# Attention weights turned within SBUF and divided after the value product

## The chip, the cores and the metric

The kernel runs on one core of a Trainium2 chip, in one launch. The metric is device time in microseconds, the median of the runs. A single profiled execution gives the trace; its span is the time from the first to the last instruction.

## What is computed

Two layers are applied to four images of 32 x 32 positions and 768 channels, in float32. Each layer normalises in 32 channel groups, runs multi-head attention with decomposed relative position terms (12 heads of 64 channels, 1024 queries and 1024 keys per image), projects, and adds the input. Cut to the attention, with S = 1024:

```python
q, k, v = (x_normed @ Wqkv)                     # per head: S x 64
bias = rel_h[..., :, None] + rel_w[..., None, :]   # from q and two small tables
scores = scale * q @ k.T + bias                 # S x S
attn = softmax(scores, axis=-1)
out = attn @ v
x = x + out @ Wproj + bproj
```

The second layer scales q once more before the position terms and has a bias on q, k and v.

## The kernel before

Data lie with channels on the 128 partitions. An image's attention is done by pairs of heads: head 0 of a pair is on partitions 0 to 63 and head 1 on 64 to 127. There are 8 image passes (2 layers, 4 images) of 6 pairs each, so 48 pairs, numbered g, and each pair has 8 units n of 128 queries. The main loop (L491) walks the 384 units in order. The order on TensorE (PE) is written by hand; the other engines' orders and the DMA queues are laid out by the framework's scheduler, and every engine works through its own order. DMAs from SyncE's queue (SP) are issued in order, and eight completion semaphores go round over all DMAs, so that one DMA waits for the eighth before it.

One turn of the loop does this on PE: the scores of the next unit (`scores`, L320: both heads, two blocks of 512 keys), a share of the waiting projection work (`take`, L464), at some units the value product (`weigh`), and the turning of new values (`turn_values`). The projection work is that of the next pair (`project_in`, L225, six groups of six matmuls for q, k and v) and the output projection (`project_out`, L425). Whatever has been put in the list `early` runs at the beginning of the next turn, for instance the position products (`positions`, tp, L276).

For one unit and head the softmax goes through five engines:

- POOL adds the two position terms into a score buffer sc (`biases`, L308), two units ahead.
- PE writes the scores to PSUM (s; three buffers).
- VectorE (DVE) adds both, negated, and keeps the minimum (L327, sm); this frees the PSUM buffer.
- ScalarE (ACT) takes the exponential and its sum (L331).
- DVE takes the reciprocal of the sums (L335), and POOL multiplies the block with it (L338).
- DVE transposes the block in squares of 32 by 32 into tb (L356).

After two units, SP writes tb of each head to DRAM (td, 1 MB, L359), and reads it back rearranged (pt, 1 MB, L360), so that keys lie on the partitions. pt holds 512 queries of one head in a single buffer per head. Every four units `weigh` multiplies with the values: 16 matmuls of 512 columns (8 key blocks, 2 heads; each float32 matmul is two instructions in the trace), and two copies from PSUM to attn (L379).

Score buffers (pool `sc`, six of 4 KB per partition) also hold v before it is turned (L218) and the result t of the position products (L280). ACT sends t to DRAM (tdr, L283); sixteen SP transfers read it back shifted (rel, L298), and POOL's bias sums of the next pair use it. The projection of v writes its columns in a changed order (L222), which the squares of the transposes ask for. PSUM has two further buffers (`ps_m`), in which projections, turned values, value products and outputs alternate.

Of the kernel before, what the change touches and what calls it, by code (L numbers as in the profile page):

```python
# [23 lines left out]
FP = mybir.dt.float32  # L28
AF = mybir.ActivationFunctionType
ALU = mybir.AluOpType  # L30

P = 128
B, HW, C = 4, 32, 768
S = HW * HW
NH, D = 12, 64
NC = C // P
NT = S // P
# [3 lines left out]
HALF = 512  # L41
# [7 lines left out]
def attention_blocks(ctx: ExitStack, tc: tile.TileContext, a: dict, out: bass.AP):  # L49
    nc = tc.nc  # L50
# [6 lines left out]
    apool = ctx.enter_context(tc.tile_pool(name="attn", bufs=6))  # L57
    qkpool = ctx.enter_context(tc.tile_pool(name="qk", bufs=2))
    vpool = ctx.enter_context(tc.tile_pool(name="v", bufs=2))
    scpool = ctx.enter_context(tc.tile_pool(name="sc", bufs=6))  # L60
    tbpool = ctx.enter_context(tc.tile_pool(name="tb", bufs=4))
    ptpool = ctx.enter_context(tc.tile_pool(name="pt", bufs=1))
    relpool = ctx.enter_context(tc.tile_pool(name="rel", bufs=2))
    iopool = ctx.enter_context(tc.tile_pool(name="io", bufs=4))
    small = ctx.enter_context(tc.tile_pool(name="small", bufs=4))
    dram = ctx.enter_context(tc.tile_pool(name="scratch", bufs=1, space=bass.MemoryType.DRAM))
    dram2 = ctx.enter_context(tc.tile_pool(name="scratch2", bufs=2, space=bass.MemoryType.DRAM))
# [9 lines left out]
    NPAIR = NI * NP  # L77
# [133 lines left out]
    def project_in(g, which, i):  # L211

        im, pair = divmod(g, NP)
        l = images[im][0]
        xn, w = xn_of[im], w_of[g, which]
        cols = slice(i * HALF, (i + 1) * HALF)
        if i == 0:
            pool, tag = (scpool, "sc") if which == 2 else (qkpool, "qk"[which])  # L218
            qkv_of[g, which] = pool.tile([P, S], FP, tag=tag, name=f"{'qkv'[which]}_{g}")
        to = qkv_of[g, which][:, cols]  # L220
        if which == 2:
            to = qkv_of[g, 2].rearrange("p (k j y) -> p y k j", y=4, k=NT)[:, 2 * i : 2 * i + 2]  # L222
        t = ps_m.tile([P, HALF], FP, tag="m", name=f"pj_{g}_{which}_{i}")
        for c in range(NC):
            nc.tensor.matmul(  # L225
                t, lhsT=w[:, c, :], rhs=xn[c][:, cols],
                start=(c == 0), stop=(c == NC - 1),
            )
            if c < NC - 1:
                yield True  # L230
        if which == 2:
            t = t.rearrange("p (y k j) -> p y k j", y=2, k=NT)
        bias = bqkv[:, which, pair : pair + 1]
        if which == 0:
            if l == 0:
                nc.scalar.activation(to, t, AF.Copy, scale=SCALE)  # L236
            else:
                nc.scalar.activation(to, t, AF.Identity, bias=bias, scale=SCALE * SCALE)  # L238
        elif l == 0:
            nc.vector.tensor_copy(to, t)  # L240
        else:
            nc.vector.tensor_scalar(to, t, bias, None, ALU.add)
        if which == 0:
            early.append(lambda: positions(g, i))
        if which == 2 and i == 1:
            late.extend([lambda: turn_values(g, 0), lambda: turn_values(g, 1)])
        if i == 1 and g + 1 < NPAIR:
            early.append(lambda: load_w(g + 1, which))
        if which == 2 and i == 1 and pair == NP - 1 and im + 1 < NI:
            early.extend([lambda: load_x(im + 1), lambda: norm_stats(im + 1)])  # L250
        yield True

    def turn_values(g, i):


        if i == 0:
            v_of[g] = vpool.tile([P, NT, P], FP, tag="v", name=f"v_{g}")
        t = ps_m.tile([P, 4, P], FP, tag="m", name=f"vt_{g}_{i}")
        for j in range(4):
            at = 4 * i + j  # L260
            nc.tensor.transpose(t[:, j, :], qkv_of[g, 2][:, at * P : (at + 1) * P], ident)  # L261
        nc.scalar.copy(v_of[g][:, 4 * i : 4 * i + 4, :], t)  # L262

    def positions(g, i):
# [7 lines left out]
        for j in range(4):  # L272
            for h in range(2):
# [3 lines left out]
                    ps[:, h, j, :], lhsT=q[rows, at * P : (at + 1) * P], rhs=tabs[l][rows, :],  # L277
                    start=True, stop=True,
                )
        t = scpool.tile([P, 4, 2, P], FP, tag="sc", name=f"t_{g}_{i}")  # L280
        nc.scalar.copy(t, ps.rearrange("p h j r -> p j h r"))  # L281
        td = t_of[g]
        nc.scalar.dma_start(  # L283
# [14 lines left out]
                        nc.sync.dma_start(out=rel_of[g][32 * y : 32 * y + 32, h, ax, :, :], in_=src)  # L298


    sc_of, tb_of, pt_of, attn_of = {}, {}, {}, {}

    def biases(g, n):
        rel = rel_of[g]
        for h in range(2):
            sc = scpool.tile([P, HW, HW], FP, tag="sc", name=f"sc_{g}_{n}_{h}")
            sc_of[g, n, h] = sc
            nc.gpsimd.tensor_tensor(  # L308
                sc, rel[:, h, 0, n, :].unsqueeze(2).to_broadcast([P, HW, HW]),
                rel[:, h, 1, n, :].unsqueeze(1).to_broadcast([P, HW, HW]), ALU.add,  # L310
            )

    def scores(g, n):
        q, k = qkv_of[g, 0], qkv_of[g, 1]
        ps = [ps_s.tile([P, S], FP, tag="s", name=f"s_{g}_{n}_{h}") for h in range(2)]
        for i in range(2):
            cols = slice(i * HALF, (i + 1) * HALF)
            for h in range(2):
                rows = slice(h * D, (h + 1) * D)
                nc.tensor.matmul(  # L320
                    ps[h][:, cols], lhsT=q[rows, n * P : (n + 1) * P], rhs=k[rows, cols],
                    start=True, stop=True,
                )
        st = small.tile([P, 3, 2], FP, tag="sm", name=f"sm_{g}_{n}")
        for h in range(2):
            sc = sc_of[g, n, h].rearrange("p y x -> p (y x)")
            nc.vector.tensor_tensor_reduce(  # L327
                out=sc, in0=ps[h], in1=sc, scale=-1.0, scalar=BIG, op0=ALU.add, op1=ALU.min,
                accum_out=st[:, 0, h : h + 1],
            )  # L330
            nc.scalar.activation(  # L331
                sc, sc, AF.Exp, bias=st[:, 0, h : h + 1], scale=-1.0,
                accum_out=st[:, 1, h : h + 1],
            )
        nc.vector.reciprocal(st[:, 2, :], st[:, 1, :])  # L335
        for h in range(2):
            sc = sc_of[g, n, h].rearrange("p y x -> p (y x)")
            nc.gpsimd.tensor_scalar(sc, sc, st[:, 2, h : h + 1], 1.0, ALU.mult, ALU.mult)  # L338

    def turn(g, n):  # L340

        half, quarter, j = n // 4, n // 2 % 2, n % 2
        for h in range(2):
            if n % 4 == 0:
                pt_of[g, half, h] = ptpool.tile(  # L350
                    [P, 2, 4, NT, 2 * HW], FP, tag=f"pt{h}", name=f"pt_{g}_{half}_{h}"
                )
            if j == 0:
                tb_of[h] = tbpool.tile([P, HW, 2, HW], FP, tag="tb", name=f"tb_{g}_{n}_{h}")
            tb, pt = tb_of[h], pt_of[g, half, h]
            nc.vector.transpose(tb[:, :, j, :], sc_of[g, n, h])  # L356
            if j == 1:
                td = dram2.tile([P, S * 2], FP, tag=f"td{h}", name=f"td_{g}_{n}_{h}")
                nc.sync.dma_start(out=td, in_=tb.rearrange("p k n i -> p (k n i)"))  # L359
                nc.sync.dma_start(  # L360
                    out=pt[:, quarter].rearrange("p r k t -> p r (k t)"),
                    in_=td.rearrange("(r j) (y t) -> (j y) r t", r=4, y=4),
                )

    def weigh(g, half):
        if half == 0:
            attn_of[g] = apool.tile([P, S], FP, tag="attn", name=f"attn_{g}")
        av = ps_m.tile([P, HALF], FP, tag="m", name=f"av_{g}_{half}")
        for k in range(NT):
            for h in range(2):  # L370
                rows = slice(h * D, (h + 1) * D)
                nc.tensor.matmul(  # L372
                    av[rows, :], lhsT=v_of[g][:, k, rows],
                    rhs=pt_of[g, half, h][:, :, :, k, :].rearrange("p q r t -> p (q r) t"),
                    start=(k == 0), stop=(k == NT - 1),
                )
        for q in range(2):
            at = half * HALF + q * 2 * P
            nc.vector.tensor_copy(  # L379
                attn_of[g][:, at : at + 2 * P].rearrange("p (n r i) -> p r n i", n=2, r=4),  # L380
                av[:, q * 2 * P : (q + 1) * 2 * P].rearrange("p (r n i) -> p r n i", n=2, r=4),
            )

# [53 lines left out]

    early, late = [], []

    def run(todo):
        while todo:
            todo.pop(0)()
# [30 lines left out]
    with tc.manual_schedule(engines={mybir.EngineType.PE}):  # L477
# [13 lines left out]
        for at, (g, n) in enumerate(units):  # L491
# [12 lines left out]
            if end and pair == NP - 1 and n == 2:  # L504
                todo = put_out(im, 0, range(12))
            run(early)
            if at + 1 < len(units):
                scores(*units[at + 1])
            if at + 2 < len(units):
# [2 lines left out]
            del late[:1]  # L512
            turn(g, n)
            take(todo, -(-left(todo) // (NT - n)))
            if n % 4 == 1 and at > 4:
                weigh(*(units[at - 2][0], n // 4 ^ 1))
            run(ready)
        weigh(NPAIR - 1, 1)
        run(early)
        todo = put_out(NI - 1, 1, range(12))  # L520
        while todo:
# [49 lines left out]
```

## Time and profile before

| | |
|---|---|
| Median of 3 runs | 4029.03 us (4026.11 to 4030.14) |
| Profiled execution, its own time | 4009.88 us |
| Its span | 4008.2 us |
| Mean granted clock of TensorE | 0.98 |
| Busy share PE, DVE, POOL, ACT | 95%, 58%, 57%, 29% |
| Main DMA queue | 564720 packets, 1032.05 MB, 73.6% of 16 engines' span |

Groups of the trace are named by line, engine and operation, then output<-input. A group gives its count, its busy time in us and the mean of one in ns, then the idle time of the engine before it and who ended that. In the chain of waits each line gives start, length and what ran; "issue" is time in which the profile shows no wait. In timelines the numbers are start and length in us. SPq and ACTq are the issuing queues. A float32 matmul counts as two instructions, each with its weight load (PEld).

### The profile page before, as it was taken

The page shows a single profiled execution, that of the slowest core. Times are in us where ns is not written, and L with a number is a line of the kernel's source. Part 1 is how long each engine was busy: PE and PEld are TensorE (multiplying, and loading weights), DVE is VectorE, ACT ScalarE, POOL GpSimd, SP SyncE. Part 2 cuts the span into 40 slices and gives each one's busy share as a digit, 9 for nine tenths or more (in the row PEclk, how much of TensorE's full clock was granted, in tenths as well). Part 3 has the DMA queues.
Part 4 walks back from the last instruction along what each step waited for, and adds up shares of the span by engine and source line. Part 5 has one row for each costly group of instructions (what it writes and reads, how often), then busy time and mean ns, then how long its engine had stood idle before and what let it go on. Part 6 is the DMA issues. An engine that isn't in the chain of part 4 may idle for free.

```text
span 4008.2 us, 39298 instructions
## 1 busy us (share of the span) xinstructions
PE 3795.4 (95%) x13056; PEld 1577.2 (39%) x13056; DVE 2324.9 (58%) x3520; ACT 1150.5 (29%) x1848; POOL 2300.8 (57%) x1555
## 2 busy tenths in 40 slices
PE   7989899999999999999999998999999999999998
PEld 3334333433344334444344343433344343434332
DVE  4555655547565565656665566555665566546653
ACT  2233223322232222322232223323233222322320
POOL 4656556655666546656556565655556565556661
PEclk9999999999999999999999999999999999999998
DMA  4777777878787787877877787878877788778867
GB/s 166 247 260 266 284 257 278 299 248 290 257 288 276 260 300 253 295 268 278 285 275 277 266 298 280 278 251 288 301 264 265 266 287 305 261 248 283 288 250 244
DMA packets 615612, 1084.89 MB, mean 271 GB/s; under 512 B 234481, under 2 KB 295153, under 8 KB 566257
## 3 DMA queue, kind: packets, MB, share of 16 engines
q1 hardware_dynamic: 564720, 1032.05, 73.6%
q10 hardware_dynamic: 50688, 50.34, 3.7%
q8 instruction: 103, 1.69, 0.2%
q14 instruction: 101, 0.82, 0.1%
HBM read 578.92 MB, written 503.32 MB: 270 GB/s over the span
## 4 chain that ended last, share of the span: by engine, by line
PE 61%; DMA 11%; DVE 10%; POOL 6%; ACT 5%; issue 5%; SPq 1%; ACTq 0%; DVEq 0%; POOLq 0%
PE pj L225 20%; PE av L372 17%; PE s L320 11%; PE o L425 9%; DMA tdr<-t 8%; DVE tb L356 4%; ACT sc L331 4%; POOL sc L308 3%; POOL sc L338 3%; DVE sc L327 3%; PE tp L276 3%; DMA pt<-td 2%; DVE st L155 1%; ACT t L281 1%; PE vt L261 1%
## 5 line engine op out<-in xcount | busy, mean ns | idle before, releaser
L308 POOL TENSOR_TENSOR sc<-rel 128x1024 f32<-128x1024 f32 x768 | 1451.6, 1910 | 578.2 <-DMA tdr<-t 341.4
L225 PE MATMUL pj<-xn,w 128*128 128x512 f32 x3456 | 1581.4, 607 | 1.1 <-DVE xn L201 1.1
L331 ACT ACTIVATE sc<-sc,sm 128x1024 f32<-128x1024 f32 x768 | 878.6, 1145 | 2063.0 <-DVE sm L327 1558.6
L338 POOL TENSOR_SCALAR sc<-sc,sm 128x1024 f32<-128x1024 f32 x768 | 849.1, 1118 | 1063.1 <-DVE sm L335 1028.8
L356 DVE STREAM_TRANSPOSE tb<-sc 128x1024 f32<-128x1024 f32 x768 | 917.9, 1226 | 741.5 <-POOL sc L338 740.3
L225 PEld LDWEIGHTS pj<-xn,w 128*128 128x128 f32 x3456 | 640.3, 192 | 924.5 <-issue 908.9
L327 DVE CUSTOM_DVE_ANT_0 sc<-s,sc 128x1024 f32<-128x1024 f32 x768 | 905.8, 1214 | 159.3 <-PE s L320 155.8
L320 PE MATMUL s<-k,q 64*128 64x512 f32 x3072 | 844.7, 623 | 54.3 <-DVE sm L327 54.3
L372 PE MATMUL av<-pt,v 128*64 128x512 f32 x3072 | 706.9, 606 | 34.1 <-DMA pt<-td 10.2
L425 PE MATMUL o<-attn,wo 128*128 128x512 f32 x1152 | 537.6, 615 | 26.3 <-DVE res L432 21.2
L320 PEld LDWEIGHTS s<-k,q 64*128 64x128 f32 x3072 | 294.0, 189 | 461.0 <-issue 288.7
L372 PEld LDWEIGHTS av<-pt,v 128*64 128x64 f32 x3072 | 264.4, 139 | 462.6 <-issue 369.1
L425 PEld LDWEIGHTS o<-attn,wo 128*128 128x128 f32 x1152 | 213.2, 193 | 333.8 <-issue 272.2
L335 DVE RECIPROCAL sm<-sm 128x2 f32<-128x2 f32 x384 | 63.5, 165 | 441.5 <-ACT sc L331 441.5
L379 DVE COPY attn<-av 128x256 f32<-128x256 f32 x192 | 71.9, 416 | 251.1 <-PE av L372 251.0
L281 ACT COPY t<-tp 128x1024 f32<-128x1024 f32 x96 | 97.1, 1012 | 285.4 <-PE tp L276 277.9
L276 PE MATMUL tp<-tab,q 64*128 64x128 f32 x1536 | 111.6, 285 | 42.3 <-ACT q L238 20.9
L331 ACT ACTIVATION_READ_ACCUMULATOR sc<-sc,sm 128x1 f32 x768 | 143.2, 186 | 0.0
L276 PEld LDWEIGHTS tp<-tab,q 64*128 64x128 f32 x1536 | 93.3, 187 | 108.9 <-ACT q L236 40.5
L262 ACT COPY v<-vt 128x512 f32<-128x512 f32 x96 | 55.9, 583 | 219.4 <-PE vt L261 218.4
L261 PE MATMUL vt<-ident,v 128*128 128x128 f32 x384 | 60.0, 280 | 34.1 <-DVE res L432 28.8
L261 PEld LDWEIGHTS vt<-ident,v 128*128 128x128 f32 x384 | 46.1, 142 | 92.5 <-DVE res L432 40.4
(45 smaller groups left out, 655.7 us busy)
## 6 DMA issues: line engine op xcount, KB each, us to landing
td<-tb SPq DMA_DIRECT2D x384, 1024.0 KB, 6.1
pt<-td SPq DMA_DIRECT2D x384, 1024.0 KB, 7.2
w<-in_wqkv SPq DMA_DIRECT2D x144, 384.0 KB, 7.2
tdr<-t ACTq DMA_DIRECT2D x96, 512.0 KB, 7.6
rel<-tdr SPq DMA_DIRECT2D x768, 32.0 KB, 2.0
part<-res SPq DMA_DIRECT2D x96, 256.0 KB, 5.3
res<-part SPq DMA_DIRECT2D x96, 256.0 KB, 5.1
wo<-in_wo SPq DMA_DIRECT2D x84, 192.0 KB, 4.4
```

Source lines behind the costliest of these rows:

```text
L225: nc.tensor.matmul(t, lhsT=w[:, c, :], rhs=xn[c][:, cols], start=(c == 0), stop=(c == NC - 1),)
L261: nc.tensor.transpose(t[:, j, :], qkv_of[g, 2][:, at * P : (at + 1) * P], ident)
L276: nc.tensor.matmul(ps[:, h, j, :], lhsT=q[rows, at * P : (at + 1) * P], rhs=tabs[l][rows, :], start=True, stop=True,)
L281: nc.scalar.copy(t, ps.rearrange("p h j r -> p j h r"))
L308: nc.gpsimd.tensor_tensor(sc, rel[:, h, 0, n, :].unsqueeze(2).to_broadcast([P, HW, HW]), rel[:, h, 1, n, :].unsqueeze(1).to_broadcast([P, ...
L320: nc.tensor.matmul(ps[h][:, cols], lhsT=q[rows, n * P : (n + 1) * P], rhs=k[rows, cols], start=True, stop=True,)
L327: nc.vector.tensor_tensor_reduce(out=sc, in0=ps[h], in1=sc, scale=-1.0, scalar=BIG, op0=ALU.add, op1=ALU.min, accum_out=st[:, 0, h : h + 1],)
L331: nc.scalar.activation(sc, sc, AF.Exp, bias=st[:, 0, h : h + 1], scale=-1.0, accum_out=st[:, 1, h : h + 1],)
L338: nc.gpsimd.tensor_scalar(sc, sc, st[:, 2, h : h + 1], 1.0, ALU.mult, ALU.mult)
L356: nc.vector.transpose(tb[:, :, j, :], sc_of[g, n, h])
L372: nc.tensor.matmul(av[rows, :], lhsT=v_of[g][:, k, rows], rhs=pt_of[g, half, h][:, :, :, k, :].rearrange("p q r t -> p (q r) t"), start=(k ...
L425: nc.tensor.matmul(t, lhsT=w[:, c - c0, :], rhs=attn_of[im * NP + c][:, cols], start=(c == c0), stop=(c == c1 - 1),)
```

## The change

- The blocks are no longer divided before the value product. POOL's multiplication (L338) goes; the reciprocal is taken once per 256 queries over both heads. It is written to DRAM (rd) and read back onto all 64 partitions of each head (rb), and the value product is multiplied with it when it leaves PSUM.
- The transposed blocks no longer pass through DRAM. Both heads and two units share one tb; sixteen transfers of 32 rows by 4 KB move its four row blocks into the four row blocks of pt, within SBUF. pt now holds 256 queries of both heads, in two buffers.
- `weigh` works on 256 queries, every two units, with 16 matmuls of 256 columns and one multiplication.
- v is written in its own order. v and t have a pool of their own (`tmp`); `sc` has three buffers of both heads.
- From the second pair of an image on, the position products go to a list `later`, which runs one turn after `early` would.

```diff
-    scpool = ctx.enter_context(tc.tile_pool(name="sc", bufs=6))
-    tbpool = ctx.enter_context(tc.tile_pool(name="tb", bufs=4))
-    ptpool = ctx.enter_context(tc.tile_pool(name="pt", bufs=1))
+    scpool = ctx.enter_context(tc.tile_pool(name="sc", bufs=3))
+    tmppool = ctx.enter_context(tc.tile_pool(name="tmp", bufs=2))
+    tbpool = ctx.enter_context(tc.tile_pool(name="tb", bufs=2))
+    ptpool = ctx.enter_context(tc.tile_pool(name="pt", bufs=2))
+    rbpool = ctx.enter_context(tc.tile_pool(name="rb", bufs=3))
...
-            pool, tag = (scpool, "sc") if which == 2 else (qkpool, "qk"[which])
+            pool, tag = (tmppool, "tmp") if which == 2 else (qkpool, "qk"[which])
...
-        if which == 2:
-            to = qkv_of[g, 2].rearrange("p (k j y) -> p y k j", y=4, k=NT)[:, 2 * i : 2 * i + 2]
...
-            early.append(lambda: positions(g, i))
-        if which == 2 and i == 1:
-            late.extend([lambda: turn_values(g, 0), lambda: turn_values(g, 1)])
+            (later if pair else early).append(lambda: positions(g, i))
+        if which == 2:
+            late.append(lambda: turn_values(g, i))
...
-        t = scpool.tile([P, 4, 2, P], FP, tag="sc", name=f"t_{g}_{i}")
+        t = tmppool.tile([P, 4, 2, P], FP, tag="tmp", name=f"t_{g}_{i}")
...
-        nc.vector.reciprocal(st[:, 2, :], st[:, 1, :])
-        for h in range(2):
-            sc = sc_of[g, n, h].rearrange("p y x -> p (y x)")
-            nc.gpsimd.tensor_scalar(sc, sc, st[:, 2, h : h + 1], 1.0, ALU.mult, ALU.mult)
...
     def turn(g, n):
-            nc.vector.transpose(tb[:, :, j, :], sc_of[g, n, h])
-            if j == 1:
-                td = dram2.tile([P, S * 2], FP, tag=f"td{h}", name=f"td_{g}_{n}_{h}")
-                nc.sync.dma_start(out=td, in_=tb.rearrange("p k n i -> p (k n i)"))
-                nc.sync.dma_start(
-                    out=pt[:, quarter].rearrange("p r k t -> p r (k t)"),
-                    in_=td.rearrange("(r j) (y t) -> (j y) r t", r=4, y=4),
-                )
+        quarter, j = divmod(n, 2)
+        if j == 0:
+            tb_of[g, quarter] = tbpool.tile([P, 4, 2, NT, 2, HW], FP, tag="tb", name=f"tb_{g}_{n}")
+        tb = tb_of[g, quarter]
+        for h in range(2):
+            nc.vector.transpose(
+                tb[:, :, h, :, j, :].rearrange("p y k i -> p k y i"),
+                sc_of[g, n][:, h].rearrange("p (k y) x -> p k y x", y=4),
+            )
+        if j == 1:
+            pt = ptpool.tile([P, 4, 2, NT, 2 * HW], FP, tag="pt", name=f"pt_{g}_{quarter}")
+            st = st_of[g, quarter]
+            nc.vector.reciprocal(
+                st[:, 2].rearrange("p h n -> p (h n)"), st[:, 1].rearrange("p h n -> p (h n)")
+            )
+            rd = dram2.tile([2, 2 * P], FP, tag="rd", name=f"rd_{g}_{quarter}")
+            nc.sync.dma_start(
+                out=rd.rearrange("h (n p) -> p (h n)", p=P),
+                in_=st[:, 2].rearrange("p h n -> p (h n)"),
+            )
+            rb = rbpool.tile([P, 2 * P], FP, tag="rb", name=f"rb_{g}_{quarter}")
+            for y in range(4):
+                for r in range(4):
+                    nc.sync.dma_start(
+                        out=pt[32 * y : 32 * y + 32, r].rearrange("p h k t -> p (h k t)"),
+                        in_=tb[32 * r : 32 * r + 32, y].rearrange("p h k n i -> p (h k n i)"),
+                    )
+            for h in range(2):
+                nc.sync.dma_start(
+                    out=rb[h * D : (h + 1) * D, :], in_=rd[h : h + 1, :].to_broadcast([D, 2 * P])
+                )
 
-    def weigh(g, half):
+    def weigh(g, quarter):
...
-                    rhs=pt_of[g, half, h][:, :, :, k, :].rearrange("p q r t -> p (q r) t"),
+                    rhs=pt_of[g, quarter][:, :, h, k, :],
...
-        for q in range(2):
-            at = half * HALF + q * 2 * P
-            nc.vector.tensor_copy(...)
+        at = quarter * 2 * P
+        nc.vector.tensor_tensor(
+            attn_of[g][:, at : at + 2 * P].rearrange("p (n r i) -> p n r i", n=2, r=4),
+            av.rearrange("p (r n i) -> p n r i", n=2, r=4),
+            rb_of[g, quarter].rearrange("p (n r i) -> p n r i", n=2, r=4), ALU.mult,
+        )
...
             run(early)
+            early, later = later, early
...
-            if n % 4 == 1 and at > 4:
-                weigh(*(units[at - 2][0], n // 4 ^ 1))
+            if n % 2 == 1 and at > 2:
+                weigh(units[at - 2][0], units[at - 2][1] // 2)
```

More of the change, by code (lines that the diff above doesn't have):

```diff
@@ L230, in project_in @@
                 yield True
-        if which == 2:
-            t = t.rearrange("p (y k j) -> p y k j", y=2, k=NT)
         bias = bqkv[:, which, pair : pair + 1]
@@ L298, in positions @@
                         nc.sync.dma_start(out=rel_of[g][32 * y : 32 * y + 32, h, ax, :, :], in_=src)
-    sc_of, tb_of, pt_of, attn_of = {}, {}, {}, {}
+    sc_of, st_of, tb_of, pt_of, rb_of, attn_of = {}, {}, {}, {}, {}, {}
     def biases(g, n):
         rel = rel_of[g]
+        sc = scpool.tile([P, 2, HW, HW], FP, tag="sc", name=f"sc_{g}_{n}")
+        sc_of[g, n] = sc
         for h in range(2):
-            sc = scpool.tile([P, HW, HW], FP, tag="sc", name=f"sc_{g}_{n}_{h}")
-            sc_of[g, n, h] = sc
             nc.gpsimd.tensor_tensor(
-                sc, rel[:, h, 0, n, :].unsqueeze(2).to_broadcast([P, HW, HW]),
+                sc[:, h], rel[:, h, 0, n, :].unsqueeze(2).to_broadcast([P, HW, HW]),
                 rel[:, h, 1, n, :].unsqueeze(1).to_broadcast([P, HW, HW]), ALU.add,
@@ L323, in scores @@
                 )
-        st = small.tile([P, 3, 2], FP, tag="sm", name=f"sm_{g}_{n}")
+        if n % 2 == 0:
+            st_of[g, n // 2] = small.tile([P, 3, 2, 2], FP, tag="sm", name=f"sm_{g}_{n}")
+        st = st_of[g, n // 2]
         for h in range(2):
-            sc = sc_of[g, n, h].rearrange("p y x -> p (y x)")
+            sc = sc_of[g, n][:, h].rearrange("p y x -> p (y x)")
             nc.vector.tensor_tensor_reduce(
                 out=sc, in0=ps[h], in1=sc, scale=-1.0, scalar=BIG, op0=ALU.add, op1=ALU.min,
-                accum_out=st[:, 0, h : h + 1],
+                accum_out=st[:, 0, h, n % 2 : n % 2 + 1],
@@ L330, in scores @@
             )
             nc.scalar.activation(
-                sc, sc, AF.Exp, bias=st[:, 0, h : h + 1], scale=-1.0,
-                accum_out=st[:, 1, h : h + 1],
-            )
-        nc.vector.reciprocal(st[:, 2, :], st[:, 1, :])
-        for h in range(2):
[L337 to L347, printed above, removed]
-        for h in range(2):
-            if n % 4 == 0:
-                pt_of[g, half, h] = ptpool.tile(
-                    [P, 2, 4, NT, 2 * HW], FP, tag=f"pt{h}", name=f"pt_{g}_{half}_{h}"
-                )
[L353 to L356, printed above, removed]
-            if j == 1:
-                td = dram2.tile([P, S * 2], FP, tag=f"td{h}", name=f"td_{g}_{n}_{h}")
-                nc.sync.dma_start(out=td, in_=tb.rearrange("p k n i -> p (k n i)"))
-                nc.sync.dma_start(
-                    out=pt[:, quarter].rearrange("p r k t -> p r (k t)"),
-                    in_=td.rearrange("(r j) (y t) -> (j y) r t", r=4, y=4),
-                )
@@ L365, in weigh, with turn @@
-    def weigh(g, half):
-        if half == 0:
+                sc, sc, AF.Exp, bias=st[:, 0, h, n % 2 : n % 2 + 1], scale=-1.0,
+                accum_out=st[:, 1, h, n % 2 : n % 2 + 1],
+            )
+    def turn(g, n):
+        quarter, j = divmod(n, 2)
+        if j == 0:
+            tb_of[g, quarter] = tbpool.tile([P, 4, 2, NT, 2, HW], FP, tag="tb", name=f"tb_{g}_{n}")
+        tb = tb_of[g, quarter]
+        for h in range(2):
+            nc.vector.transpose(
[4 more added lines that the diff above has]
+            pt = ptpool.tile([P, 4, 2, NT, 2 * HW], FP, tag="pt", name=f"pt_{g}_{quarter}")
+            pt_of[g, quarter] = pt
+            st = st_of[g, quarter]
[8 more added lines that the diff above has]
+            rb = rbpool.tile([P, 2 * P], FP, tag="rb", name=f"rb_{g}_{quarter}")
+            rb_of[g, quarter] = rb
+            for y in range(4):
[7 more added lines that the diff above has]
+                    out=rb[h * D : (h + 1) * D, :], in_=rd[h : h + 1, :].to_broadcast([D, 2 * P])
+                )
@@ L367, in weigh @@
+    def weigh(g, quarter):
+        if quarter == 0:
             attn_of[g] = apool.tile([P, S], FP, tag="attn", name=f"attn_{g}")
-        av = ps_m.tile([P, HALF], FP, tag="m", name=f"av_{g}_{half}")
+        av = ps_m.tile([P, HALF], FP, tag="m", name=f"av_{g}_{quarter}")[:, : 2 * P]
         for k in range(NT):
@@ L373, in weigh @@
                     av[rows, :], lhsT=v_of[g][:, k, rows],
-                    rhs=pt_of[g, half, h][:, :, :, k, :].rearrange("p q r t -> p (q r) t"),
+                    rhs=pt_of[g, quarter][:, :, h, k, :],
                     start=(k == 0), stop=(k == NT - 1),
                 )
-        for q in range(2):
-            at = half * HALF + q * 2 * P
[L379 to L382, printed above, removed]
+        at = quarter * 2 * P
[4 more added lines that the diff above has]
+        )
     parts = [(im, p, o, i) for im in range(NI) for p in range(2) for o in range(NC) for i in range(2)]
@@ L437, in project_out @@
         yield True
-    early, late = [], []
+    early, later, late = [], [], []
     def run(todo):
@@ L514, in attention_blocks @@
             take(todo, -(-left(todo) // (NT - n)))
-            if n % 4 == 1 and at > 4:
-                weigh(*(units[at - 2][0], n // 4 ^ 1))
+            if n % 2 == 1 and at > 2:
+                weigh(units[at - 2][0], units[at - 2][1] // 2)
             run(ready)
-        weigh(NPAIR - 1, 1)
+        weigh(NPAIR - 1, 3)
         run(early)
```

## The prediction

> **What bounds the kernel now.** I read the page first (busy shares and groups), then the timeline of TensorE (PE) over the whole span, the chain of waits around one of its gaps, and the timeline of SP's queue. The page:
>
> ```profile
> PE 3795.4 (95%) x13056; PEld 1577.2 (39%) x13056; DVE 2324.9 (58%) x3520; ACT 1150.5 (29%) x1848; POOL 2300.8 (57%) x1555
> ...
> PE 61%; DMA 11%; DVE 10%; POOL 6%; ACT 5%; issue 5%; SPq 1%; ACTq 0%; DVEq 0%; POOLq 0%
> ...
> L338 POOL TENSOR_SCALAR sc<-sc,sm 128x1024 f32<-128x1024 f32 x768 | 849.1, 1118 | 1063.1 <-DVE sm L335 1028.8
> ...
> L356 DVE STREAM_TRANSPOSE tb<-sc 128x1024 f32<-128x1024 f32 x768 | 917.9, 1226 | 741.5 <-POOL sc L338 740.3
> ```
>
> PE is the bound, yet the chain that ended last lies on it for 61% only. POOL's 849 us of division matter for one reason: DVE's transposes wait 740 us for them. The timeline of PE shows what a unit costs (a unit is 128 queries of one head pair):
>
> ```profile
> 2034.53 7.09 PE L372 MATMUL av<-pt,v 128*64 128x512 f32 x32
> ...
> 2042.14 1.16 PE L276 MATMUL tp<-tab,q 64*128 64x128 f32 x16
> ...
> 2050.29 1.99 PE L320 MATMUL s<-k,q 64*128 64x512 f32 x8
> 2052.21 5.42 PE L225 MATMUL pj<-xn,w 128*128 128x512 f32 x12
> 2057.56 1.12 PE L320 MATMUL s<-k,q 64*128 64x512 f32 x2
> 2059.65 1.98 PE L320 MATMUL s<-k,q 64*128 64x512 f32 x6 [0.97 <-DVE sm L327]
> ```
>
> Start to start, undisturbed: scores 1.92 us, six projection matmuls 5.35, values of 512 queries 7.02 (16 pairs of instructions at 0.43, the two heads together, and 0.16 of change-over). At 2057.56 a score run stops after two of its eight instructions. The chain of waits there:
>
> ```profile
> 2047.52 1.24 ACT sc L331 x2
> 2048.77 3.64 issue
> 2052.41 1.91 POOL sc L308
> 2054.32 1.11 POOL sc L338
> ...
> 2055.45 1.13 DVE tb L356
> ...
> 2058.45 1.13 DVE sc L327
> ...
> 2059.65 1.98 PE s L320 x6
> ```
>
> POOL stands 3.64 us before a bias sum (its buffer is held by t until tdr lands at 2052.35); the division queues behind that sum, the transposes behind the division, the next scores' reduction behind the transposes, and PE behind that. Even without the 3.64 us, DVE's reduction repeats every 8.40 us (2005.23, 2013.63), against 1.92 + 5.35 = 7.27 on PE.
>
> I went through PE's whole timeline, subtracting the undisturbed pace from each run of matmuls. 160 runs lose over 1 us, 297 us together: 123 in scores behind L327, 43 where tp or vt follow at once on ACT's copy of q, 37 behind the output sums L432 and L434, 94 elsewhere. Of each about 0.2 is ordinary change-over, so 265 us are stalls, and a PE without them would end near 3743.
>
> **Removed.** The division (768 x 1118 ns on POOL) with its link in the chain. The transposes then wait for the exponential alone. In the same rows: reduction at 0, first exponential 1.33 to 2.48, transposes from about 2.6 to 5.0, a copy of 0.7: 5.7 us per unit instead of 8.4, below PE's 7.27. The t tiles leave the score buffers, so the 3.64 us goes too. Of the 123 us I keep 15 (first pairs, image ends). The deferred positions put a unit between ACT's copy and tp in five pairs of six: of 43 I keep 8. Of 37 I keep 27, since those sit at image ends, where DVE computes statistics (12 x 662 ns). Of 94 I keep 50. That removes 197, less about 23 of ordinary change-over in those runs: 174. If all stalls go it is 265; if half, 132.
>
> Off the path, counted at nothing: 192 fewer reciprocals (165 ns, 32 us of DVE) and 96 plain copies of v at the 685 ns of k's copies instead of 1.08 us (38 us). PE hides them, and without that cover the 70 us would be gain.
>
> **Added.** 96 more groups of value matmuls: 96 x 0.16 = 15 us on the path. Half the columns should take half the time. The nearest row is tp: 16 instructions with 16 loads in 1.0 us, 0.125 per pair, below the 0.215 needed. The division on leaving PSUM takes the place of two copies of 416 ns per 512 queries; L434, a sum of 512 columns from PSUM with an SBUF operand, takes 674 ns, so some 0.4 for 256: equal. Transposes still write runs of 32 elements: 1226 ns stays.
>
> Moved: per 256 queries, SP issued two td and two pt of 1 MB. Now it issues one rd (512 elements of 4 bytes), sixteen pt of 32 rows by 4 KB, two rb. In the program each DMA waits for the eighth before it, so eight at most fly. What queues behind: w, rel, res, wo and stores. The built order has the rel batch ahead of the second quarter's pt in 35 pairs, and that is the tight place (the queues of ACT and SP, in order of time):
>
> ```profile
> 39.49 0.37 ACTq L283 DMA_DIRECT2D tdr<-t  x1
> ...
> 42.41 7.74 SPq L298 DMA_DIRECT2D rel<-tdr  x16
> ...
> 2044.39 0.37 ACTq L283 DMA_DIRECT2D tdr<-t  x1
> ...
> 2052.35 7.73 SPq L298 DMA_DIRECT2D rel<-tdr  x16
> 2060.19 0.86 SPq L359 DMA_DIRECT2D td<-tb  x2
> 2064.26 3.37 SPq L360 DMA_DIRECT2D pt<-td  x2
> ```
>
> From tp's start: 2.25 us to tdr's issue, 2.9 to land alone (8.0 beside 2 MB of pt), 0.4 for a w, 7.73 for rel, 0.35 for rd: pt starts at 13.7 (18.7). PE reaches that quarter's values at 1.0 + 1.8 + 5.35 + 3.6, then two units of 7.27, in the new order 26.3. So sixteen transfers have 12.6 us (7.6), and the first value applies, the earlier quarter having landed. Their price is in no row. Below: two td of 1 MB, issued at 2060.19, have both landed 7.1 us later, when the second pt goes. Above: two rounds of eight at the slowest pt<-td landing, 10.9 each: 21.8. I take two rounds at the 5.1 us of the 256 KB res loads and the rd, 11 us, being nearest in size. That stalls nothing; for pairs where tdr is late or a res load slips behind the batch I put 20 us in all. rb lands during the 3.6 us of value matmuls.
>
> [...]
>
> **Sum.** 4008.2 - 174 + 15 + 20 = 3869 of span; the profiled execution took 4009.9, 19 us below the median of 4029.0. The same difference, 139, gives 3890. The likeliest case's own range: all stalls gone 3780; half gone and 70 us of late pt 3980.
>
> **Rivals.** A, slower: pt comes late. Each us over 12.6 is paid in 35 pairs, and DVE's division blocks its queue as well. The gain of 159 is spent at 12.6 + 4.5 = 17 us; at 20 it is +259 - 159, some 4130. For it: no SBUF to SBUF row, eight in flight, SP busier. Against: halves of the work now crossing DRAM twice go away (384 x 1 MB each way, 73.6% of the DMA engines), and other quarters have over 20 us. B, slower: halved matmuls don't halve, since two loads of 139 ns must follow each other: 0.278 instead of 0.215 for 3072 pairs, +194, some 4080. Against: the loads of both heads lie side by side in the trace, and tp's pace. C: the stalls move rather than vanish, because DVE's order still holds PE or pt takes 14 to 17 us: 3980 to 4040.
>
> **Chances.** Forecast 0.62, A 0.17, B 0.07, C 0.14. About 0.2%, 8 us, is what a measurement of this kernel can tell from no change. Faster 0.62 + 0.09 of C = 0.71, same 0.05, slower 0.24. The range 3790 to 4080 leaves out most of A and the case of nearly no stalls.
>
> **What would show it.** Right: no L338 row, transposes released by ACT, score runs of 1.92 us without a stop, the reduction's period equal to PE's, POOL near 37%, value runs of about 3.6 us, and 16 pt issued in some 8 us. Wrong: value runs waiting for pt after rel (A), value runs of 4.5 us with loads one after the other (B), score runs still behind DVE (C).

## The result and the profile after

The changed kernel takes 4464.5 us (median of 4 runs, 4451.0 to 4467.6) against 4027.6: a ratio of 1.1081, with a 95% interval of 1.1055 to 1.1107. It is slower by 437 us where I forecast 139 us of gain.

The page of the changed kernel: busy time, the shares of the chain that ended last, and the groups of the value products and of DVE's transposes (busy time and mean ns, then idle time in front and who ended it).

```profile
PE 3877.5 (87%) x16128; PEld 1832.2 (41%) x16128; DVE 2285.9 (51%) x3328; ACT 1152.6 (26%) x1848; POOL 1454.8 (33%) x787
...
DMA 40%; PE 33%; SPq 21%; issue 4%; DVE 1%; ACT 1%; DVEq 0%; ACTq 0%
...
L382 PE MATMUL av<-pt,v 128*64 128x256 f32 x6144 | 869.9, 446 | 454.3 <-DMA rb<-rd 291.0
L346 DVE STREAM_TRANSPOSE tb<-sc 128x1024 f32<-128x1024 f32 x768 | 918.2, 1229 | 496.5 <-DMA rb<-rd 342.7
```

The chain has left PE (61% before) for transfers and for SP's queue, and 454 us of PE's idle time stand in front of the value products, 414 of them ended by rb (291.0) and pt (122.8). In all, PE's idle time grew by 373 us (212.8 to 586.3) and its busy time by 82 (3795.4 to 3877.5); together they are the 456 us by which the span grew from 4008.2 to 4463.8. The stalls that I wanted to remove are gone all the same: PE waits 0.6 us in scores behind DVE's reduction, where it was 54.3, and 6.7 us in tp behind ACT, where it was 42.3. The scores, before and after:

```profile
L320 PE MATMUL s<-k,q 64*128 64x512 f32 x3072 | 844.7, 623 | 54.3 <-DVE sm L327 54.3
L315 PE MATMUL s<-k,q 64*128 64x512 f32 x3072 | 755.2, 609 | 0.6 <-DVE sm L325 0.6
```

So the kernel won what was planned and lost more elsewhere. PE runs at a mean granted clock of 0.934 (0.98 before).

One batch, first in SP's timeline and then in the chain of waits, shows how:

```profile
2225.55 0.40 SPq L93 DMA_DIRECT2D w<-in_wqkv  x1
2226.04 0.38 SPq L358 DMA_DIRECT2D rd<-sm  x1
2226.52 13.85 SPq L366 DMA_DIRECT2D pt<-tb  x16
2240.41 1.23 SPq L371 DMA_DIRECT2D rb<-rd  x2
```

```profile
2226.04 8.71 DMA rd<-sm
2234.77 0.51 SPq L366
2235.33 0.59 SPq L366
...
2241.05 2.11 DMA rb<-rd
2243.20 5.15 PE av L382 x32
```

rd, the 2 KB of reciprocals, is issued in 0.38 us and lands 8.7 us later. The eighth DMA behind it, a pt, waits for it (SP stands 501.9 us in all in pt behind rd), the remaining pt leave at 0.6 us each, then rb, then the values. The batch takes 13.9 us here; over all 192 batches the median is 15.8, and half lie between 14.4 and 18.5. That happens four times per pair, beside 8 us of rel and some 10 of w, wo, res and stores. SP spends 2902 us on issuing and 1191 on waiting for transfers, 92% of the span: its queue is full.

### The profile page after: what moved, and what is told of

The parts are those of the page before. It is cut to its first block, busy times and chain, and to the rows that moved or that the text cites. A ratio compares the mean times of both kernels' runs of the same rounds, so it can differ in the third digit from the quotient of the medians.

```text
span 4463.8 us, 47650 instructions
## 1 busy us (share of the span) xinstructions
PE 3877.5 (87%) x16128; PEld 1832.2 (41%) x16128; DVE 2285.9 (51%) x3328; ACT 1152.6 (26%) x1848; POOL 1454.8 (33%) x787
## 4 chain that ended last, share of the span: by engine, by line
DMA 40%; PE 33%; SPq 21%; issue 4%; DVE 1%; ACT 1%; DVEq 0%; ACTq 0%
DMA rd<-sm 16%; SPq L366 13%; PE av L382 10%; PE pj L224 9%; DMA pt<-tb 7%; PE s L315 6%; PE o L435 6%; SPq L293 4%; DMA tdr<-t 4%; DMA part<-res 4%; DMA rb<-rd 2%; DMA out<-res 2%; SPq L371 2%; DMA mid<-res 2%; PE tp L271 1%
## 5 line engine op out<-in xcount | busy, mean ns | idle before, releaser
L382 PE MATMUL av<-pt,v 128*64 128x256 f32 x6144 | 869.9, 446 | 454.3 <-DMA rb<-rd 291.0
L382 PEld LDWEIGHTS av<-pt,v 128*64 128x64 f32 x6144 | 547.3, 162 | 837.2 <-issue 640.6
L315 PE MATMUL s<-k,q 64*128 64x512 f32 x3072 | 755.2, 609 | 0.6 <-DVE sm L325 0.6
L435 PE MATMUL o<-attn,wo 128*128 128x512 f32 x1152 | 565.7, 641 | 99.8 <-DMA wo<-in_wo 38.0
L315 PEld LDWEIGHTS s<-k,q 64*128 64x128 f32 x3072 | 265.6, 186 | 305.2 <-issue 301.7
L388 DVE TENSOR_TENSOR attn<-av,rb 128x256 f32<-128x256 f32 x192 | 81.4, 424 | 483.5 <-PE av L382 467.7
L442 DVE SCALAR_TENSOR_TENSOR res<-o,bo,res 128x512 f32<-128x512 f32 x96 | 70.2, 732 | 95.7 <-PE o L435 55.9
L444 DVE TENSOR_TENSOR res<-o,res 128x512 f32<-128x512 f32 x96 | 64.4, 671 | 28.8 <-DMA res<-part 21.0
L237 DVE COPY k<-pj 128x512 f32<-128x512 f32 x48 | 33.1, 689 | 86.3 <-PE pj L224 86.3
L239 DVE TENSOR_SCALAR k<-pj,bqkv 128x512 f32<-128x512 f32 x48 | 35.9, 748 | 68.8 <-PE pj L224 68.8
```

The lines of the kernel that those rows point to most:

```text
L315: nc.tensor.matmul(ps[h][:, cols], lhsT=q[rows, n * P : (n + 1) * P], rhs=k[rows, cols], start=True, stop=True,)
L382: nc.tensor.matmul(av[rows, :], lhsT=v_of[g][:, k, rows], rhs=pt_of[g, quarter][:, :, h, k, :], start=(k == 0), stop=(k == NT - 1),)
L435: nc.tensor.matmul(t, lhsT=w[:, c - c0, :], rhs=attn_of[im * NP + c][:, cols], start=(c == c0), stop=(c == c1 - 1),)
```

## The experiments

Theory T1, as first put: rd's landing costs, through the DMAs that wait for it. Rival T2: the sixteen transfers are slow. Medians in us; the kernel before ran beside each group (e1 to e4, e5 to e8, e9 to e12, e13 to e15: 4027.6, 4026.9, 4015.6, 4029.9).

| run | us | ratio to before, 95% interval |
|---|---|---|
| e1 rd as 128-byte rows | 3898.7 | 0.9684 (0.9663 to 0.9706) |
| e2 half of the bytes moved | 4339.1 | 1.0780 (1.0754 to 1.0806) |
| e3 as e1, move through DRAM | 4552.6 | 1.1309 (1.1288 to 1.1330) |
| e4 before, deferral alone | 3976.1 | 0.9872 (0.9848 to 0.9896) |
| e5 rd last, rb later | 4813.9 | 1.1963 (1.1929 to 1.1997) |
| e6 as e1, rb one unit later | 3874.3 | 0.9618 (0.9600 to 0.9635) |
| e7 as e6, pt from two queues | 3793.0 | 0.9417 (0.9400 to 0.9433) |
| e8 before, no division | 3967.6 | 0.9844 (0.9821 to 0.9866) |
| e9 rd as 128 rows of 16 B | 3899.5 | 0.9706 (0.9678 to 0.9734) |
| e10 rd from ACT's queue | 5171.6 | 1.2869 (1.2829 to 1.2909) |
| e11 rd from POOL's queue | 4656.1 | 1.1587 (1.1555 to 1.1619) |
| e12 pt from two queues alone | 4294.1 | 1.0682 (1.0650 to 1.0715) |
| e13 as e1, dummy write, 512 x 4 B | 4621.1 | 1.1467 (1.1444 to 1.1491) |
| e14 as e1, dummy write, 128 x 16 B | 3957.5 | 0.9806 (0.9781 to 0.9830) |
| e15 before, no division, deferral | 3842.4 | 0.9533 (0.9517 to 0.9549) |

### Is it rd? (e1, e9)

e1 turns the reciprocals before they are written:

```diff
-            nc.vector.reciprocal(st[:, 2]..., st[:, 1]...)
-            rd = dram2.tile([2, 2 * P], FP, tag="rd")
-            nc.sync.dma_start(out=rd.rearrange("h (n p) -> p (h n)", p=P), in_=st[:, 2]...)
+            rc = rcs[quarter % 2]                       # two constant [128, 32] tiles
+            nc.vector.reciprocal(rc[:, 0:4], st[:, 1]...)
+            nc.vector.transpose(rt, rc)
+            rd = dram2.tile([HW, P], FP, tag="rd")
+            nc.sync.dma_start(out=rd.rearrange("c (b i) -> b c i", i=HW), in_=rt)
```

> Edit: the reciprocals of 256 queries are turned by one 32 x 32 transpose on DVE, and rd is written as 128 rows of 128 B where it was 512 elements of 4 B; rb in two buffers to make room. As many DMAs as before, the same order. Theory T1 (SP's queue is the bound, because in each batch the eighth DMA after rd waits for rd, which lands some 8.7 us after its issue): the batch of 14 to 17 us shrinks by about 4.4 us to 10 to 12, four times per pair, so 18 of 93 us per pair; SP is no bound any more and the time falls to PE's pace, 3880 to 3960. [...]

3898.7: T1, and 566 us below the changed kernel. In the page of e1 the chain is back on PE, and the idle time in front of the values is 75 us instead of 454:

```profile
PE 79%; SPq 11%; DMA 6%; DVE 2%; issue 2%; ACT 1%; DVEq 0%
...
L389 PE MATMUL av<-pt,v 128*64 128x256 f32 x6144 | 721.7, 388 | 75.2 <-DMA rb<-rd 45.2
```

Here rd is 128 elements of 128 B, 16 KB in all, of which rb reads 2. e9 keeps bytes, place and queue, and changes the shape alone; rb then reads the reciprocals in a wrong order, so e9 measures the shape and is no kernel to use:

```diff
-            rd = dram2.tile([2, 2 * P], FP, tag="rd")
-            nc.sync.dma_start(out=rd.rearrange("h (n p) -> p (h n)", p=P), in_=st[:, 2]...)
+            rd = dram2.tile([P, 4], FP, tag="rd")
+            nc.sync.dma_start(out=rd, in_=st[:, 2]...)
```

> The changed kernel with rd written as 128 rows of 16 B, each partition's four reciprocals together; rb then reads the same bytes in a wrong order, so the value products are divided by other rows' sums (that much of the computation is changed). Bytes, count and place of the DMAs are those of the changed kernel, only the 512 elements have become 128. T1 with the element count as the cause of the 8.7 us: rd lands in some 2 to 4 us, the wait of the eighth DMA goes, 3880 to 3960. Rival (small writes to DRAM are slow by their size, or it was the transpose's 128 B rows that helped): 4200 or more.

3899.5, as e1. The same 2 KB in 128 elements instead of 512 do no harm (4464.5 in the changed kernel). The DMA lists give count, size and the median from issue to landing: first e5, which has 512 elements, then e9:

```profile
w<-in_wqkv SPq DMA_DIRECT2D x144, 384.0 KB, 10.7
rd<-sm SPq DMA_DIRECT2D x192, 2.0 KB, 9.1
```

```profile
w<-in_wqkv SPq DMA_DIRECT2D x144, 384.0 KB, 3.6
rd<-sm SPq DMA_DIRECT2D x192, 2.0 KB, 3.3
```

rd itself lands in 9.1 or 3.3 us, and a weight load of 384 KB needs 10.7 us in e5, where 127 of the 144 stand right behind rd, and 3.6 in e9, where pt stand behind rd.

### Who waits, or who is held? (e5, e10, e11, e12, then e13, e14)

If the wait of the eighth DMA were all, another place or another queue would help. e5 issues rd behind the sixteen pt, and rb two units later:

```diff
+        if j == 1:
+            run(backs)                                  # the rb of the quarter before
...
-            nc.sync.dma_start(out=rd..., in_=st[:, 2]...)       # ahead of the 16 pt
+            nc.sync.dma_start(out=rd..., in_=st[:, 2]...)       # behind them
-            for h in range(2): nc.sync.dma_start(out=rb..., in_=rd...)
+            backs.append(...)                           # the same two DMAs
```

> The changed kernel with rd still written as 512 elements of 4 B, but issued after the sixteen pt, and rb issued two units later, just ahead of the next quarter's batch or behind the w between. No instruction is added or taken away. T1 (the wait of every eighth DMA behind rd in SP's order is what costs, since rd lands 8.7 us after its issue): nothing stands behind the wait any more, the batch takes 16 x 0.6 = 10 us, and the time comes near the 3899 of the 128-byte rows: 3880 to 3960. Rival (512 elements of 4 B are costly for the DMA engines themselves and hold up the transfers around them wherever they stand): 4100 or more.

4813.9: T1 in that form fell. rb now stands at the head of SP's queue until rd has landed (800.3 us), and DVE waits 833 us for rb before it can multiply.

e10 and e11 change the queue of rd alone:

```diff
-            nc.sync.dma_start(out=rd..., in_=st[:, 2]...)
+            nc.scalar.dma_start(out=rd..., in_=st[:, 2]...)     # e10
+            nc.gpsimd.dma_start(out=rd..., in_=st[:, 2]...)     # e11
```

> The changed kernel with rd, still 512 elements of 4 B, issued from ACT's queue. It stays in the round of eight completion semaphores that SP's pt also use. T1 (the wait for the semaphore of rd): the eighth pt still waits, 4300 to 4470. Rival (what costs is that transfers behind rd in SP's own queue stand behind its 512 packets: the w right behind rd took 10.7 us to land in the run with rd last): the wait goes, 3900 to 4000.

5171.6, outside both expectations. SP stands 880.7 us in pt and 648.8 in rb behind rd; the issue of rd on ACT waits for the reciprocal. Whether exponentials behind that issue lose time by it, and how the excess over the changed kernel comes about, I did not separate.

> The changed kernel with rd, still 512 elements of 4 B, issued from POOL's queue. Its completion is counted by semaphores of its own, so no pt waits for it; rb, behind the batch, does. T1 (wait of the eighth): batch 10 us, 3880 to 3960, unless POOL's order puts rd late behind bias sums (1.9 us each), which then shows as rb waiting: up to 4050. If the 512 elements hold the DMA engines themselves: 4150 or more.

4656.1. None of SP's waits is for rd here, and it is slower still, which speaks for the last sentence of the expectation. rd lands in 9.4 us.

> The changed kernel with every second pt issued from ACT's queue, rd as in the change. T1: the eighth DMA after rd comes sooner (8 x 0.3 us) and still waits until 8.7 us; the batch takes 11 to 12 us instead of 14 to 17, SP's queue has 4 us more per 256 queries and is just below PE's pace: 3880 to 4050, ACT's waits included. Rival (SP's 16 issues of 0.59 us as such are the bound, not rd): about the 3793 of the run that has both.

```diff
-                    nc.sync.dma_start(out=pt..., in_=tb...)
+                    (nc.sync if r % 2 == 0 else nc.scalar).dma_start(out=pt..., in_=tb...)
```

4294.1, above the expectation: relief of SP's queue returns 170 of the 566 us.

e13 and e14 settle it. To the mended kernel e1 they add a write that nobody waits for and nobody reads:

```diff
+            rx = dram2.tile([4, P], FP, tag="rx")                              # e13
+            nc.gpsimd.dma_start(out=rx.rearrange("c p -> p c"), in_=rc[:, 0:4])
+            rx = dram2.tile([P, 4], FP, tag="rx")                              # e14
+            nc.gpsimd.dma_start(out=rx, in_=rc[:, 0:4])
```

> The kernel of the 128-byte rows, and beside it, per 256 queries, the same reciprocals are written once more as 512 elements of 4 B from POOL's queue to memory that nobody reads. No pt, rb or matmul waits for this write; its completion is counted apart. If the 512 elements hold the DMA engines for some 9 us, so that whatever is in flight lands late, this alone gives back most of the loss: 4350 to 4650. If only the waits for rd's completion cost (T1 as first put), it stays at 3899 to 3930.

> As e13, the second write as 128 rows of 16 B. Both theories: 3899 to 3930; it prices POOL's issue (0.77 us in front of a bias sum) and one more transfer, so that the difference between e13 and e14 is the element count alone.

4621.1 and 3957.5 (27 us above its expectation). The difference, 664 us, is the shape of that write alone: 3.5 us for each of the 192 writes. With the count, the size of an element (4 B against 16) and the order of the targets in DRAM change as well; no run separates the three, though e1's 128 elements carried eight times the bytes and were harmless. The DMA lists of e13, then of e14, give ACT's queue (q10: packets, MB, share of the 16 engines' span) and rx:

```profile
q10 hardware_dynamic: 50688, 50.34, 8.4%
rx<-rc POOLq DMA_DIRECT2D x192, 2.0 KB, 8.8
```

```profile
q10 hardware_dynamic: 50688, 50.34, 4.1%
rx<-rc POOLq DMA_DIRECT2D x192, 2.0 KB, 2.7
```

e13, in POOL's timeline, and the chain's longest pieces beside it:

```profile
2222.78 0.77 POOL L370 DMA_DIRECT2D rx<-rc  x1
2259.95 0.78 POOL L370 DMA_DIRECT2D rx<-rc  x1
```

```profile
2223.11 8.89 DMA pt<-tb
2261.41 10.15 DMA tdr<-t
```

The chain of e14 has this for a pt:

```profile
2208.41 2.37 DMA pt<-tb
```

A pt on SP's queue that sets out right behind rx needs 8.9 us, a tdr on ACT's queue 10.2 (the medians in e9 are 3.3 and 3.7), though neither depends on it. T1 must read so: while the small write is under way, for some 9 us, transfers of the other two queues are late as well; the waits for rd are only one way in which that shows. In the changed kernel the DMA engines moved 79 GB/s from 2230.4 to 2234.8, late in rd's flight, with SP waiting as well; in e9, from 2242 to 2246 of a batch whose rd went at 2239.43, 203 to 221.

It is not the landing alone that comes late: the same packets and bytes of ACT's queue occupied 8.4% of the engines' span in e13 and 4.1% in e14, so there the packets themselves took longer too. By what mechanism no run here shows.

### The transfers and the queue (e2, e6, e7)

e2 moves head 0's half of each row, and both products read it:

```diff
-                        out=pt[32 * y : 32 * y + 32, r]..., in_=tb[32 * r : 32 * r + 32, y]...
+                        out=pt[32 * y : 32 * y + 32, r, 0]..., in_=tb[32 * r : 32 * r + 32, y, 0]...
-                    rhs=pt_of[g, quarter][:, :, h, k, :],
+                    rhs=pt_of[g, quarter][:, :, 0, k, :],
```

> Leaves out part of the computation: only head 0's half of each row (2 KB of 4 KB) is moved, and both heads' value products read it; every DMA and every instruction stays. T1 (issue and rd): an issue costs its 0.59 us whatever the length, and rd still holds the eighth: batch 13 to 15 us, time 4350 to 4460. T2 (the transfers' rate): 64 KB need half the time, the issue falls to about 0.3 us and the batch to 11 or 12 (rd's 8.7 us and then eight at 0.3), time 4000 to 4150.

The median issue of a pt is 588 ns against 589, the median batch 16.3 us against 15.8: T2 falls, the bytes do not set the pace of the issue. The time is 4339.1, 125 us below the changed kernel and 11 less than the least I had for T1; where the 125 us come from I did not separate.

e6 is e1 with the two rb in the list of e5, run one unit later; e7 adds the edit of e12.

```diff
+        run(backs)                                      # at the start of every turn
         quarter, j = divmod(n, 2)
...
-            for h in range(2): nc.sync.dma_start(out=rb..., in_=rd...)
+            backs.append(...)                           # the same two DMAs
```

> The kernel of the 128-byte rows with rb issued one unit later. There SP waits 230 us at rb, the eighth DMA after tdr, and PE 45 us for rb. T1: that wait moves behind pt and w to a place where tdr has landed; 3860 to 3890. Rival: the eighth-DMA wait on tdr only moves to w, rel or pt, since SP's order has the rel batch behind it anyway: 3890 to 3905, no difference.

> As e6, and every second pt transfer is issued from ACT's queue. If SP's issue of 16 x 0.6 us still delays pt, values wait less and it is 20 to 40 us faster than e6. Rival: ACT's exponentials now stand behind its DMA issues and their waits (8 x 0.6 us per 256 queries, about 900 us in all beside 1153 of work), which delays DVE's transposes: slower than e6 by 20 to 150 us.

3874.3, within T1's range: PE's wait for rb falls from 45.2 to 11.3 us. T1's reason did not hold, though: SP's wait at rb for tdr did not go but grew, from 230.3 to 324.9 us, and PE is merely held by it less. And e7 takes 3793.0, 5.8% below the kernel before: the second queue gives 81 us, where I had expected 20 to 40 or a loss; ACT does wait (297 us before exponentials, behind pt issues), but its spare time covers that. PE is the bound again:

```profile
PE 3686.7 (97%) x16128; PEld 1705.8 (45%) x16128; DVE 2324.2 (61%) x3520; ACT 1152.0 (30%) x1848; POOL 1455.7 (38%) x789
...
PE 91%; DMA 3%; DVE 2%; issue 2%; ACT 1%; SPq 0%; ACTq 0%; DVEq 0%
```

### The parts by themselves (e3, e4, e8, e15)

e3 has, for the sixteen pt of e1, one td write and four reads:

```diff
+            nc.sync.dma_start(out=td.rearrange("r j y t -> (r j) (y t)"), in_=tb...)
+            for y in range(4):
+                nc.sync.dma_start(out=pt[32 * y : 32 * y + 32]..., in_=td[:, :, y].rearrange("r j t -> j r t"))
```

> As e1, and the move goes through DRAM again: one write of tb (2 MB) and four reads of 512 KB in place of the sixteen transfers of 32 rows. Everything else of the change stays (no division on POOL, value products per 256 queries, deferred positions). T1 and T2 both expect SP's queue to be free (five issues instead of sixteen) and the score stalls to stay away: 3870 to 3960, as the sum without the move gives. If the moved bytes as such are the bound (2 MB each way per quarter), values wait for pt and it stays above 4000.

4552.6, above 4000 as the last sentence allowed, though neither theory expected it: PE waits 605.1 us for pt, SP 542.4 us for td to land before it can read it back, and 542.3 us at rb for rd. Against this form of the detour (one write, then four reads into 32 partitions each) the move within SBUF is worth 654 us (e3 less e1).

e4 and e8 are edits of the kernel before; e15 has both.

```diff
-            early.append(lambda: positions(g, i))                              # e4
+            (later if pair else early).append(lambda: positions(g, i))
...
             run(early)
+            early, later = later, early
...
-        nc.vector.reciprocal(st[:, 2, :], st[:, 1, :])                         # e8
-        for h in range(2):
-            nc.gpsimd.tensor_scalar(sc, sc, st[:, 2, h : h + 1], 1.0, ALU.mult, ALU.mult)
```

> The kernel before with one part of the change alone: the position products go one turn later from the second pair of an image on. My tally of PE's stalls put 43 us on tp and vt behind ACT's copy of q, of which 35 would go: 3985 to 4005. Rival: the later tdr makes the rel batch and so the next pair's bias sums late, and the score stalls behind DVE grow by as much: 4020 to 4060.

> The kernel before without the reciprocals and POOL's multiplication (the division is left out altogether); DRAM detour, 512-query values and early positions stay. My sum kept 15 of 123 us behind DVE's reduction and 50 of 94 elsewhere once the division is gone: by it some 110 to 150 us go, 3880 to 3920. Rival: the stalls move, because position products still stand right behind ACT's copy and t still holds score buffers: 3960 to 4010.

> The kernel before without reciprocals and division (left out) and with the position products one turn later: both parts of the stall sum with the DRAM detour and 512-query values kept. The two alone gave 60 and 51 us. If they add up as my sum of 174 assumes: 3850 to 3920. Rival: with the stalls gone, values wait for pt through DRAM (114 us there without the division), so the two do not add up: 3920 to 3960, and the move within SBUF is a part of the gain.

51.5 us for the deferral (its time is 9 us below the expected range) and 59.3 for the division, where the rival's number was right and its reason only in part: tp still waits 33.6 us for ACT, but the values wait 113.9 for pt. Together 187.5, more than the sum of both, and again 8 us below the range. PE's page line and its value group in e15:

```profile
PE 3703.1 (96%) x13056; PEld 1507.9 (39%) x13056; DVE 2300.2 (60%) x3136; ACT 1152.5 (30%) x1848; POOL 1457.7 (38%) x787
...
L368 PE MATMUL av<-pt,v 128*64 128x512 f32 x3072 | 732.0, 603 | 50.2 <-DMA pt<-td 49.4
```

So the stalls can go without any move within SBUF; e15 does not pay for a division anywhere, though.

## Why the prediction was wrong, point by point

- **The bound, and the 174 us of stalls: right.** Two parts alone, in the kernel before, brought 187.5 us (e15). Their split was not: I gave the division 108 us and the deferral 35; alone they brought 59 and 52, probably because either leaves a stall that holds the other's. So the total came out better than its parts, which is partly luck.
- **15 us for more groups, values at half the time: right.** What follows an undisturbed value run starts 3.60 us after it (e7); rival B did not occur.
- **16 pt in 11 us, late pt 20 us: right in size, not in kind.** With rd mended an undisturbed batch takes 10.1 us (2235.94 to 2246.01 in e1; the median is 11.0; I had hoped for 8 of issue), and PE waits 15.8 us for pt. But it is the issue, 0.59 us each with rows of 4 KB and of 2 KB alike (median 589 ns in the changed kernel, 588 in e2), and not two rounds of landing.
- **rd: the step that failed.** I counted its issue, 0.35 us, and let rb land beside the values. I had written that each DMA waits for the eighth before it, and did not apply it to the pt that comes eighth behind rd. I bounded pt from both sides because the trace had no such row, and did not do so for rd, of which the trace had no row either. 512 elements of 4 B land after some 9 us (8.71 in the batch shown, median 9.1 in e5), and transfers on other queues are late meanwhile (8.9 us for a pt and 10.2 for a tdr in e13, where the medians in e9 are 3.3 and 3.7). That is 566 us (changed kernel less e1), 2.9 for each of 192; e13 less e14 gives 3.5. Of the 566, 164 are a longer busy time of PE (3877.5 against 3713.4 us), at a granted clock of 0.934 instead of 0.982; the rest is PE's idle time.
- **rb hidden: no; nearly, once rd is mended.** PE waits 291 us for rb in the changed kernel; in e1 its place costs 24 us (e1 less e6).
- **SP's sum: never made.** I named what the batch is queued ahead of, but did not add up SP's pair. With 14 to 17 us for a batch it is 4 x 14 to 17, rd and rb 6, rel 8, the rest about 10: 80 to 92 us, against 81 per pair at the forecast's pace (3869 / 48). With my own 11 us it would have been 68 and would have warned of nothing: the sum fails only by rd. Even with rd mended the queue still cost 81 us (e6 less e7).
- **Rival A** had the side and the place (values waiting for pt), with the wrong price (4130) and condition: not 35 quarters behind rel, but all quarters, behind rd. **C** had two conditions: the stalls did not move to DVE, but its batch of 14 to 17 us is about what came (median 15.8), for a reason that it did not name and at more than its price (3980 to 4040).
- **The sum itself** without rd: 3869 of span forecast, 3896.4 in e1, 27 above, of which rb is 24.

## What to carry to other kernels

Here the price of a DMA depended on how its bytes were cut and not on their sum alone: 2 KB landed in 9.1 us as 512 elements of 4 B (e5) and in 3.3 as 128 of 16 B (e9). Transfers beside it on other queues paid as well (8.9 us for a pt in e13, 2.4 in e14). A side path of 2 KB deserves the same two-sided bound as the 2 MB beside it. Give small per-row values a row shape (four neighbours, or a 32 x 32 transpose: 3899.5 and 3898.7 us here, against 4464.5) before they leave SBUF. When one transfer becomes sixteen, add up the issuing queue's whole period and compare it with the bound engine's; a second queue may be worth more than the order within one (here 81 us, e6 less e7, against 24, e1 less e6).

## What the runs showed of the hardware

- 2 KB from SBUF to DRAM as 512 elements of 4 B took 9.1 us from issue to landing, as 128 elements of 16 B 3.3 us (e5, e9), and POOL's queue was no better (9.4 in e11).
- While such a write was under way, a 128 KB move within SBUF on another queue took 8.9 us, where one in e14 took 2.4 (e13, e14); the packets of ACT's queue, the same in number and bytes, took 8.4% of the engines' span instead of 4.1%.
- The issue of a 32-row transfer within SBUF took 0.59 us with rows of 4 KB (changed kernel) and of 2 KB (e2) alike; the 1 MB read pt<-td of the kernel before took 0.37.
- The same 16128 matmul instructions were busy for 3877.5 us at a granted clock of 0.934 in the changed kernel and 3713.4 us at 0.982 in e1; a value run that had waited 5.3 us took 5.15 us (at 2243.20, at a granted clock of 0.71), an undisturbed one 3.67 (at 2229.17 in e1, at 1.00).
